# One third of a depthwise convolution moved from TensorE to ScalarE and GpSimd, in a kernel of dilated attention and binary convolution

## The chip, the cores and the metric

The kernel runs on one core of a Trainium2 chip, in float32 throughout except for the softmax weights, which are carried as three bfloat16 terms. The metric is the device time of one execution in microseconds (us), as the median of several runs. One execution was also taken by the hardware profiler; the profile that is shown below is of that execution. Engines are named as the profile names them: PE is TensorE's matmul, PEld its weight load, DVE is VectorE, ACT is ScalarE, POOL is GpSimd, SP is the engine whose queue issues nearly all transfers.

## The reference

The input x has the shape (16, 56, 56, 384): 16 images of 56 by 56 pixels with 384 channels. Two layers follow each other, each with a group norm ahead of it (32 groups of 12 channels, over all pixels of an image) and a residual sum behind it.

```python
# layer 0: dilated attention
x = x + attention(gn(x), w_qkv, w_proj, b_proj)
#   qkv = w_qkv applied per pixel; 3 groups of 128 channels with dilation 1, 2, 3;
#   4 heads of 32 channels per group; each pixel attends to its 9 dilated neighbours
# layer 1: depthwise 3x3 convolution with a binary kernel
x = x + conv(gn(x), w)
#   w_clip = clip(w, -1, 1);  k = w_clip + (sign(w_clip) - w_clip)
#   conv_general_dilated(x, k, padding='SAME', feature_group_count=384)
```

The change touches the second layer: every channel is convolved alone, with nine taps whose values are the signs of its weights.

## The kernel before, in words

**Tiling.** An image is cut into 7 slices of 8 rows (`PX` = 448 pixels); there are 112 slices in all. The channels lie on the partitions, as 3 groups of 128 (`NG`, index `g` or `j`). Three stages are run as a pipeline over slices, with scratch arrays in HBM between them. Stage A (`plan_a`) loads x, turns it by TensorE transposes, takes the sums for the first norm and writes `xd`. Stage B (`plan_b`) reads `xd` back, normalises it, computes k, v and q by matmuls of 128 x 448 (`pkv`, `pq`, line 337), multiplies q with three shifted views of k on DVE (`t`, L387), sums them over a head's channels on TensorE (`ps`, L371), takes the softmax, and then weighs v: for each of 27 pairs of group and tap a matmul spreads the weights over the partitions (`pb_a`, L443), DVE multiplies them with a shifted view of v (`w`, L446), and GpSimd adds the product to the group's sum (`y`, L453). The output projection (`po`, L467) and the residual follow, the sums for the second norm, and `x1d` is written. Stage C (`plan_c`) is the convolution.

**The convolution.** For each group j of 128 channels, `load` brings 4 sets of 32 channels into a tile `z` of 96 partitions. Each set lies there three times, shifted by one row (three transfers, L531). ScalarE normalises the four sets (L536). `convolve` then runs 12 matmuls for the group, three column shifts by four sets, with diagonal kernels `kdiag` of 96 x 32 as weights (L553). The profile counts each float32 matmul as two. The four sets of a shift go to different columns of the array, and the code keeps the twelve back to back. DVE adds the result to the slice of `x1d` that `load_x` brought (L560). `turn` transposes the sum back, ScalarE copies it out of PSUM (`osb`, L567), and a transfer writes it to the output.

**The order.** Pieces of the stages are entered in a table by a step and a rank (`at(when, order, piece)`), 9 steps to a slice; stage C of a slice runs 10 slices behind its stage B. The sorted table is only the order of priority. A scheduler places the instructions of each engine from it, by its own estimate of when they are ready, and the hardware then executes each engine's instructions in that order. DVE, ACT, POOL and the SP queue each wait at the head of their own line; so does PE for its matmuls.

**Buffers that the change and the prediction touch.** The pool `w_p` has 5 tiles: the DVE product five places later needs the tile that POOL's sum frees. `ps_bc` has 2 PSUM banks for `pb_a`. `ps_mt` has 4 banks, shared by most other matmul results. `z_p` has 3 tiles. Keys and values lie in `kv`, with `KV_SLOTS` = 3 slots by slice; besides its own 8 rows a slot has the halo rows above and below, copied by transfers between slots (L350, L351). `mr` holds mean and scale of a norm by channel, `mrz` the same in the layout of `z`.

Of the kernel before, what the change touches and what calls it, by code (L numbers as in the profile page):

```python
# [8 lines left out]
F32 = mybir.dt.float32  # L9
# [15 lines left out]
GN_CH = 12  # L25
GN_G = 32
NR = NG * HEADS * NTAP
KV_SLOTS = 3
TERMS = 3


# [1 line left out]
def dilated_attention_then_binary_conv(  # L33
# [24 lines left out]

    nc = tc.nc
    B, H, W, C = x.shape
    PX = ROWS * W
# [3 lines left out]
    SCALE = float(HD) ** -0.5  # L67
    DIL = (1, 2, 3)
    K3 = 3 * HD

    xf = x.rearrange("b h w c -> b (h w) c")
    of = out.rearrange("b h w c -> b (h w) c")
# [51 lines left out]

    spread = const.tile([NR, NTAP, P], BF16, name="spread")

    kdiag = const.tile([K3, 3, NG * NQ, HD], F32, name="kdiag")
    with tc.tile_pool(name="setup", bufs=1) as setup:
        wq_in = setup.tile([P, 9, C], F32, name="wq_in")
        nc.sync.dma_start(wq_in, w_qkv.rearrange("(t p) c -> p t c", p=P))  # L130
# [37 lines left out]
            )  # L168
        nc.vector.tensor_copy(spread, spread_f)


        kc = setup.tile([K3, 3, NG * NQ], F32, name="kc")
        nc.vector.tensor_scalar(kc, k_in, -1.0, 1.0, op0=ALU.max, op1=ALU.min)
        kp = setup.tile([K3, 3, NG * NQ], F32, name="kp")
        nc.vector.tensor_single_scalar(kp, kc, 0.0, op=ALU.is_gt)
        kn = setup.tile([K3, 3, NG * NQ], F32, name="kn")
        nc.vector.tensor_single_scalar(kn, kc, 0.0, op=ALU.is_lt)
        nc.vector.tensor_sub(kp, kp, kn)
        nc.vector.tensor_sub(kp, kp, kc)
        nc.vector.tensor_add(kp, kc, kp)  # L180
        eye3 = setup.tile([K3, HD], F32, name="eye3")
        nc.gpsimd.memset(eye3, 0.0)
        for ky in range(3):
# [4 lines left out]
        for kx in range(3):  # L188
            nc.vector.tensor_tensor(
                kdiag[:, kx],  # L190
                kp[:, kx].unsqueeze(2).to_broadcast([K3, NG * NQ, HD]),
                eye3.unsqueeze(1).to_broadcast([K3, NG * NQ, HD]),
                ALU.mult,
            )

# [8 lines left out]
    y_p = ctx.enter_context(tc.tile_pool(name="y_p", bufs=5))  # L204
    s_p = ctx.enter_context(tc.tile_pool(name="s_p", bufs=1))
    a_p = ctx.enter_context(tc.tile_pool(name="a_p", bufs=4))
    z_p = ctx.enter_context(tc.tile_pool(name="z_p", bufs=3))
    x1_p = ctx.enter_context(tc.tile_pool(name="x1_p", bufs=2))
    o_p = ctx.enter_context(tc.tile_pool(name="o_p", bufs=2))
    st_p = ctx.enter_context(tc.tile_pool(name="st_p", bufs=2))  # L210


    kv = []
    for g, d in enumerate(DIL):
        kv.append([])
        for s in range(KV_SLOTS):
            t = const.tile([P, 2, ROWS + 2 * d, W + 2 * d], F32, name=f"kv_{g}_{s}")
            nc.gpsimd.memset(t[:, :, :, 0:d], 0.0)
            nc.gpsimd.memset(t[:, :, :, W + d : W + 2 * d], 0.0)
            kv[g].append(t)  # L220

    def rows(ap):
        return ap.rearrange("p (r w) -> p r w", w=W)
# [97 lines left out]
    def plan_b(m, t0):  # L321

        b, c = divmod(m, NCH)
        slot, prev = m % KV_SLOTS, (m - 1) % KV_SLOTS
        had = {}

        def load_x():
# [12 lines left out]

        def k_or_v(g, which):

            d, cur, bef = DIL[g], kv[g][slot][:, which], kv[g][prev][:, which]
            pk = ps_mt.tile([P, 512], F32, tag="mt", name="pkv")
            project(pk, (1 + which) * C + g * P)
            nc.scalar.copy(cur[:, d : d + ROWS, d : d + W], rows(pk[:, :PX]))  # L346
            if c == 0:
                nc.gpsimd.memset(cur[:, 0:d, :], 0.0)
            else:
                nc.sync.dma_start(cur[:, 0:d, :], bef[:, ROWS : ROWS + d, :])  # L350
                nc.sync.dma_start(bef[:, ROWS + d : ROWS + 2 * d, :], cur[:, d : 2 * d, :])  # L351
            if c == NCH - 1:
                nc.gpsimd.memset(cur[:, ROWS + d : ROWS + 2 * d, :], 0.0)
# [24 lines left out]
        def score(i):  # L378

            g, ky = divmod(i, 3)  # L380
            d = DIL[g]
            qg = rows(had["q"][:, :PX])
            q3 = bass.AP(qg.tensor, qg.offset, [qg.ap[0], (0, 3), *qg.ap[1:]])
            kw = kv[g][slot][:, 0, ky * d : ky * d + ROWS, 0:W]
            k3 = bass.AP(kw.tensor, kw.offset, [kw.ap[0], (d, 3), *kw.ap[1:]])
            t = t_p.tile([P, 3, PX], F32, tag="t", name="t")
            nc.vector.tensor_tensor(t.rearrange("p k (r w) -> p k r w", w=W), q3, k3, ALU.mult)  # L387
            ready.extend((i * 3 + kx, t[:, kx, :]) for kx in range(3))
            if len(ready) >= NQ or i == 8:
                score_round()  # L390
# [47 lines left out]
        def weigh(p):  # L438

            g, o = divmod(p, NTAP)  # L440
            d, (ky, kx) = DIL[g], divmod(o, 3)
            pb = ps_bc.tile([P, 512], F32, tag="bc", name="pb_a")
            nc.tensor.matmul(pb[:, :PX], spread[:, o, :], had[f"a{g}"], start=True, stop=True)  # L443
            w = w_p.tile([P, PX], F32, tag="w", name="w")
            vw = kv[g][slot][:, 1, ky * d : ky * d + ROWS, kx * d : kx * d + W]
            nc.vector.tensor_tensor(rows(w), rows(pb[:, :PX]), vw, ALU.mult)  # L446
# [6 lines left out]
            nc.gpsimd.tensor_tensor(y, had["w0"] if o == 1 else y, w, ALU.add)  # L453
# [23 lines left out]
        def norm():  # L477
            mr = spread_stats(group_stats(stats1.pop(b)))

            mr1[b] = mrz = st_p.tile([K3, NG, NQ, 2], F32, tag="mrz", name="mrz")  # L480
            for ky in range(3):
                for q in range(NQ):
                    nc.sync.dma_start(mrz[ky * HD : (ky + 1) * HD, :, q, :], mr[q * HD : (q + 1) * HD, :, :])

        at(t0 - 18, LOADS, load_x)
        for j in range(NG):
# [20 lines left out]
    def plan_c(m, t0):  # L507
# [23 lines left out]
                nc.sync.dma_start(z[ky * HD : (ky + 1) * HD, :, lo:hi], by_set[:, :, q0 + lo : q0 + hi])  # L531

        def normalise(j):
            z = had[f"z{j}"]
            for q in range(NQ):
                nc.scalar.activation(  # L536
                    z[:, q], z[:, q], AF.Identity, bias=mr1[b][:, j, q, 0:1], scale=mr1[b][:, j, q, 1:2]
                )
            for edge in edges(j):
                nc.gpsimd.memset(edge, 0.0)  # L540

        def load_x():
            had["x1"] = x1 = x1_p.tile([P, NG, PX], F32, tag="x1", name="x1")
            nc.sync.dma_start(x1, chunk_of(x1d[b], c))

        def convolve(j):
            z = had.pop(f"z{j}")
# [67 lines left out]
```

## Time and profile before

| what | value |
|---|---|
| median of 3 runs | 6155.91 us (6143.2 to 6156.27) |
| the profiled execution, its own time | 6148.66 us |
| its span from the first to the last instruction | 6146.7 us |
| PE busy | 5892.8 us (96%), 30933 matmuls |
| DVE busy | 4420.6 us (72%) |
| POOL busy | 3364.3 us (55%) |
| ACT busy | 2270.5 us (37%) |
| mean granted TensorE clock | 0.961 |
| one slice, from 2000 to 4000 us (38 slices) | 52.6 us |

A busy share is an average over the whole span. A matmul's end is modelled in the trace, so the records of neighbouring matmuls overlap a little; what a group of them occupies is read from the distance between its start and the start of the next group. In a line of the list of groups, the part after the bar gives the total busy time and the mean duration of one instruction in ns, and the part after the second bar the idle time of the engine just before these instructions, with what ended it.

### The profile page before, as it was taken

How to read it: one execution, taken by the hardware profiler on the slowest of the kernel's cores; microseconds unless marked ns; L12 is line 12 of the kernel's file. 1: busy time of each engine (PE TensorE's matmuls, PEld its weight loads, DVE VectorE, ACT ScalarE, POOL GpSimd, SP SyncE). 2: the span in 40 equal slices, each digit the busy share in tenths (PEclk: the TensorE clock that was granted, in tenths of full speed). 3: DMA queues.
4: the chain of work that ended last, by engine and by line, in shares of the span. 5: the costliest groups of instructions: out<-in, count | busy, mean ns of one | idle time of the engine just before them, and what ended most of it. 6: DMA issues, size and time to landing. Idle time of an engine off the chain costs nothing. (4 is left out here: it accounts for less than half of the span.)

```text
span 6146.7 us, 90026 instructions
## 1 busy us (share of the span) xinstructions
PE 5892.8 (96%) x30933; PEld 2720.9 (44%) x30933; DVE 4420.6 (72%) x6431; ACT 2270.5 (37%) x4025; POOL 3364.3 (55%) x3375
## 2 busy tenths in 40 slices
PE   6989999999999999999999999999999999999986
PEld 3434444444444444444444444444444444444432
DVE  3767777777777777777777777777777777777760
ACT  2222333333333333334333333333334333333334
POOL 1656555555555555555555556555555555555650
PEclk7999999999999999999999999999999999999985
DMA  4323445554555455545554555555455554444445
GB/s 149 105 69 102 138 132 150 147 148 141 140 149 146 136 152 141 146 136 147 152 143 137 142 148 142 143 146 148 140 140 149 150 149 139 133 131 115 125 131 143
DMA packets 675072, 848.03 MB, mean 138 GB/s; under 512 B 179507, under 2 KB 674614, under 8 KB 674614
## 3 DMA queue, kind: packets, MB, share of 16 engines
q1 hardware_dynamic: 670608, 841.67, 48.8%
q8 instruction: 244, 4.00, 0.3%
q14 instruction: 214, 1.75, 0.1%
q10 hardware_dynamic: 4006, 0.61, 0.1%
HBM read 539.11 MB, written 231.21 MB: 125 GB/s over the span
## 5 line engine op out<-in xcount | busy, mean ns | idle before, releaser
L453 POOL TENSOR_TENSOR y<-y,w 128x448 f32<-128x448 f32 x2352 | 2675.0, 1137 | 1227.8 <-DVE w L446 1085.8
L446 DVE TENSOR_TENSOR w<-pb_a,kv 128x448 f32<-128x448 f32 x3024 | 1797.4, 616 | 479.0 <-PE pb_a L443 468.4
L337 PE MATMUL pkv<-xn,wqkvT 128*128 128x448 f32 x4032 | 1641.9, 542 | 0.0
L387 DVE TENSOR_TENSOR t<-pq,kv 128x1344 f32<-128x1344 f32 x1008 | 1545.9, 1547 | 86.6 <-PE pq L337 70.2
L337 PEld LDWEIGHTS pkv<-xn,wqkvT 128*128 128x128 f32 x4032 | 762.2, 190 | 622.7 <-issue 592.7
L536 ACT ACTIVATE z<-z,mrz 96x448 f32<-96x448 f32 x1344 | 939.2, 757 | 124.7 <-DMA z<-x1d 99.2
L553 PE MATMUL pc<-z,kdiag 96*32 96x440 f32 (+1 forms) x8064 | 924.3, 561 | 54.2 <-ACT z L536 32.0
L443 PE MATMUL pb_a<-aT,spread 108*128 108x448 bf16 x3024 | 929.5, 360 | 47.9 <-DVE w L446 38.5
L346 ACT COPY kv<-pkv 128x448 f32<-128x448 f32 x672 | 358.6, 534 | 1607.8 <-PE pkv L337 1607.4
L337 PE MATMUL pq<-xn,wqkvT 128*128 128x448 f32 x2016 | 904.5, 560 | 0.0
L467 PE MATMUL po<-y,wprojT 128*128 128x448 f32 x2016 | 828.6, 539 | 1.7 <-POOL y L453 1.7
L371 PE MATMUL ps<-t,sel 128*32 128x448 f32 x6048 | 781.1, 570 | 31.7 <-DVE var L255 15.9
L453 POOL TENSOR_TENSOR y<-w 128x448 f32<-128x448 f32 x336 | 382.9, 1139 | 724.6 <-DVE w L446 685.7
L560 DVE TENSOR_TENSOR x<-pc,x 128x448 f32<-128x448 f32 x336 | 209.8, 624 | 582.6 <-PE pc L553 581.9
L443 PEld LDWEIGHTS <-spread 108*128 108x128 bf16 x3024 | 238.0, 98 | 786.7 <-issue 730.1
L467 PEld LDWEIGHTS po<-y,wprojT 128*128 128x128 f32 x2016 | 382.1, 190 | 337.3 <-issue 305.8
L470 DVE SCALAR_TENSOR_TENSOR xr<-po,bias,xr 128x448 f32<-128x448 f32 x336 | 228.7, 681 | 407.5 <-PE po L467 401.8
L337 PEld LDWEIGHTS pq<-xn,wqkvT 128*128 128x128 f32 x2016 | 400.1, 200 | 260.8 <-issue 230.2
L553 PEld LDWEIGHTS pc<-z,kdiag 96*32 96x32 f32 x8064 | 265.7, 113 | 554.3 <-issue 463.3
L423 POOL TENSOR_TENSOR rest<-e,e 112x432 f32<-112x432 f32 x112 | 114.2, 1019 | 391.4 <-ACT e L422 375.1
L308 ACT COPY xa<-pt_x 128x448 f32<-128x448 f32 x336 | 179.0, 534 | 362.5 <-PE pt_x L304 355.0
L333 ACT ACTIVATE xn<-xn,mr 128x448 f32<-128x448 f32 x336 | 231.4, 751 | 202.8 <-DMA xn<-xd 145.9
(90 smaller groups left out, 3363.0 us busy)
## 6 DMA issues: line engine op xcount, KB each, us to landing
z<-x1d SPq DMA_DIRECT2D x912, 224.0 KB, 4.0
xin<-in_x_dram SPq DMA_DIRECT2D x112, 672.0 KB, 6.5
xd<-xa SPq DMA_DIRECT2D x336, 224.0 KB, 2.3
xn<-xd SPq DMA_DIRECT2D x112, 672.0 KB, 4.5
xr<-xd SPq DMA_DIRECT2D x112, 672.0 KB, 4.3
x1d<-xr SPq DMA_DIRECT2D x112, 672.0 KB, 3.1
x<-x1d SPq DMA_DIRECT2D x112, 672.0 KB, 5.0
out_dram<-osb SPq DMA_DIRECT2D x448, 168.0 KB, 2.3
```

What stands on the lines that cost most here:

```text
L333: nc.scalar.activation(xj, xj, AF.Identity, bias=mr0[b][:, j, 0:1], scale=mr0[b][:, j, 1:2])
L337: nc.tensor.matmul(dst[:, :PX], wqkvT[:, cc, o0 : o0 + P], had["xn"][:, cc, :], start=(cc == 0), stop=(cc == NG - 1))
L346: nc.scalar.copy(cur[:, d : d + ROWS, d : d + W], rows(pk[:, :PX]))
L371: return nc.tensor.matmul(had["ps"][32 * j : 32 * j + 32, :PX], sel[:, s0 : s0 + 32], tk, start=(i == 0), stop=(p + NQ >= NG * NTAP),)
L387: nc.vector.tensor_tensor(t.rearrange("p k (r w) -> p k r w", w=W), q3, k3, ALU.mult)
L443: nc.tensor.matmul(pb[:, :PX], spread[:, o, :], had[f"a{g}"], start=True, stop=True)
L446: nc.vector.tensor_tensor(rows(w), rows(pb[:, :PX]), vw, ALU.mult)
L453: nc.gpsimd.tensor_tensor(y, had["w0"] if o == 1 else y, w, ALU.add)
L467: nc.tensor.matmul(po[:, :PX], wprojT[:, g, j * P : (j + 1) * P], had[f"y{g}"], start=(g == 0), stop=(g == NG - 1))
L470: nc.vector.scalar_tensor_tensor(xr[:, j, :], po[:, :PX], bias[:, j : j + 1], xr[:, j, :], op0=ALU.add, op1=ALU.add)
L536: nc.scalar.activation(z[:, q], z[:, q], AF.Identity, bias=mr1[b][:, j, q, 0:1], scale=mr1[b][:, j, q, 1:2])
L553: return nc.tensor.matmul(pcr[q * HD : (q + 1) * HD, :, lo:hi], kdiag[:, kx, j * NQ + q, :], rows(z[:, q])[:, :, lo + kx - 1 : hi + kx - 1 ...
```

## The change

The convolution of the last 128 channels (j = 2) no longer uses `z`, `kdiag` and TensorE. Its slice is loaded once, 10 rows by 128 channels, into a tile `xg`. ScalarE normalises it into a padded tile `zg` and multiplies nine shifted views of it, each by the tap's sign of that channel (`taps_g`). GpSimd sums the nine products, in two additions of 1344 elements and two of 448, and adds the sum to the middle rows of `xg` in place (`sum_g`); `turn` reads them from there. The pieces have steps of their own in the table, from t0 - 4 to t0 + 8. The tile pool `m_p` for the products has two tiles of three products. The tile pool `z_p` goes from three tiles to two. Keys and values have separate tiles, with two slots for k and three for v. `mr1` keeps `mr` beside `mrz`.

```diff
-KV_SLOTS = 3
+K_SLOTS, V_SLOTS = 2, 3
...
+    JG = NG - 1
...
-    kdiag = const.tile([K3, 3, NG * NQ, HD], F32, name="kdiag")
+    ktap = const.tile([P, NTAP], F32, name="ktap")
+
+    kdiag = const.tile([K3, 3, JG * NQ, HD], F32, name="kdiag")
...
+        def binary(dst, k_raw):
...
+        binary(kp.rearrange("p k s -> p (k s)"), k_in.rearrange("p k s -> p (k s)"))
+        kg_in = setup.tile([P, NTAP], F32, name="kg_in")
+        nc.scalar.dma_start(kg_in, w_conv.rearrange("y x c m -> c (y x m)")[JG * P : (JG + 1) * P, :])
+        binary(ktap, kg_in)
...
-                kp[:, kx].unsqueeze(2).to_broadcast([K3, NG * NQ, HD]),
-                eye3.unsqueeze(1).to_broadcast([K3, NG * NQ, HD]),
+                kp[:, kx, : JG * NQ].unsqueeze(2).to_broadcast([K3, JG * NQ, HD]),
+                eye3.unsqueeze(1).to_broadcast([K3, JG * NQ, HD]),
...
-    z_p = ctx.enter_context(tc.tile_pool(name="z_p", bufs=3))
+    z_p = ctx.enter_context(tc.tile_pool(name="z_p", bufs=2))
     x1_p = ctx.enter_context(tc.tile_pool(name="x1_p", bufs=2))
+    xg_p = ctx.enter_context(tc.tile_pool(name="xg_p", bufs=2))
+    m_p = ctx.enter_context(tc.tile_pool(name="m_p", bufs=2))
     o_p = ctx.enter_context(tc.tile_pool(name="o_p", bufs=2))
...
     kv = []
-    for g, d in enumerate(DIL):
+    for which, slots in enumerate((K_SLOTS, V_SLOTS)):
         kv.append([])
-        for s in range(KV_SLOTS):
-            t = const.tile([P, 2, ROWS + 2 * d, W + 2 * d], F32, name=f"kv_{g}_{s}")
-            nc.gpsimd.memset(t[:, :, :, 0:d], 0.0)
-            nc.gpsimd.memset(t[:, :, :, W + d : W + 2 * d], 0.0)
-            kv[g].append(t)
+        for g, d in enumerate(DIL):
+            kv[which].append([])
+            for s in range(slots):
+                t = const.tile([P, ROWS + 2 * d, W + 2 * d], F32, name=f"{'kv'[which]}_{g}_{s}")
+                nc.gpsimd.memset(t[:, :, 0:d], 0.0)
+                nc.gpsimd.memset(t[:, :, W + d : W + 2 * d], 0.0)
+                kv[which][g].append(t)
+
+
+    zg = []
+    for s in range(2):
+        t = const.tile([P, ROWS + 2, W + 2], F32, name=f"zg_{s}")
+        nc.gpsimd.memset(t, 0.0)
+        zg.append(t)
...
         def k_or_v(g, which):
 
-            d, cur, bef = DIL[g], kv[g][slot][:, which], kv[g][prev][:, which]
+            d, slots = DIL[g], kv[which][g]
+            cur, bef = slots[m % len(slots)], slots[(m - 1) % len(slots)]
...
-            kw = kv[g][slot][:, 0, ky * d : ky * d + ROWS, 0:W]
+            kw = kv[0][g][m % K_SLOTS][:, ky * d : ky * d + ROWS, 0:W]
...
-            vw = kv[g][slot][:, 1, ky * d : ky * d + ROWS, kx * d : kx * d + W]
+            vw = kv[1][g][m % V_SLOTS][:, ky * d : ky * d + ROWS, kx * d : kx * d + W]
...
-            mr1[b] = mrz = st_p.tile([K3, NG, NQ, 2], F32, tag="mrz", name="mrz")
+            mrz = st_p.tile([K3, NG, NQ, 2], F32, tag="mrz", name="mrz")
             for ky in range(3):
                 for q in range(NQ):
                     nc.sync.dma_start(mrz[ky * HD : (ky + 1) * HD, :, q, :], mr[q * HD : (q + 1) * HD, :, :])
+            mr1[b] = mr, mrz
...
         def normalise(j):
-            z = had[f"z{j}"]
+            z, mrz = had[f"z{j}"], mr1[b][1]
             for q in range(NQ):
                 nc.scalar.activation(
-                    z[:, q], z[:, q], AF.Identity, bias=mr1[b][:, j, q, 0:1], scale=mr1[b][:, j, q, 1:2]
+                    z[:, q], z[:, q], AF.Identity, bias=mrz[:, j, q, 0:1], scale=mrz[:, j, q, 1:2]
...
         def load_x():
-            had["x1"] = x1 = x1_p.tile([P, NG, PX], F32, tag="x1", name="x1")
-            nc.sync.dma_start(x1, chunk_of(x1d[b], c))
+            had["x1"] = x1 = x1_p.tile([P, JG, PX], F32, tag="x1", name="x1")
+            nc.sync.dma_start(x1, chunk_of(x1d[b], c)[:, :JG])
...
+        lo, hi = (0 if c else 1), ROWS + (2 if c < NCH - 1 else 1)
+        zp = zg[m % 2]
+
+        def load_g():
+            had["xg"] = xg = xg_p.tile([P, ROWS + 2, W], F32, tag="xg", name="xg")
+            nc.sync.dma_start(
+                xg[:, lo:hi, :].rearrange("p r w -> p (r w)"),
+                x1d[b][JG * P : (JG + 1) * P, p0 + (lo - 1) * W : p0 + (hi - 1) * W],
+            )
+
+        def normalise_g():
+            if c == 0:
+                nc.gpsimd.memset(zp[:, 0], 0.0)
+            if c == NCH - 1:
+                nc.gpsimd.memset(zp[:, ROWS + 1], 0.0)
+            mr = mr1[b][0]
+            nc.scalar.activation(
+                zp[:, lo:hi, 1 : W + 1], had["xg"][:, lo:hi, :], AF.Identity,
+                bias=mr[:, JG, 0:1], scale=mr[:, JG, 1:2],
+            )
+
+        def taps_g(ky):
+            t = m_p.tile([P, 3, PX], F32, tag="m", name="m")
+            for kx in range(3):
+                o = 3 * ky + kx
+                nc.scalar.activation(
+                    rows(t[:, kx]), zp[:, ky : ky + ROWS, kx : kx + W], AF.Copy, scale=ktap[:, o : o + 1]
+                )
+            if ky == 0:
+                had["m"] = t
+            else:
+                nc.gpsimd.tensor_tensor(had["m"], had["m"], t, ALU.add)
+
+        def sum_g(kx):
+            t = had["m"]
+            if kx < 3:
+                nc.gpsimd.tensor_tensor(t[:, 0], t[:, 0], t[:, kx], ALU.add)
+            else:
+                mid = had["xg"][:, 1 : ROWS + 1, :].rearrange("p r w -> p (r w)")
+                nc.gpsimd.tensor_tensor(mid, t[:, 0], mid, ALU.add)
+
         def turn(s):
             pt = ps_mt.tile([P, 512], F32, tag="mt", name="pt_o")
+            mid = had["xg"][:, 1 : ROWS + 1, :].rearrange("p r w -> p (r w)")
             for j in range(NG):
-                nc.tensor.transpose(pt[:SUB, j * P : (j + 1) * P], had["x1"][:, j, s * SUB : (s + 1) * SUB], ident)
+                src = mid if j == JG else had["x1"][:, j]
+                nc.tensor.transpose(pt[:SUB, j * P : (j + 1) * P], src[:, s * SUB : (s + 1) * SUB], ident)
             osb = o_p.tile([SUB, C], F32, tag="osb", name="osb")
             nc.scalar.copy(osb, pt[:SUB, :C])
             nc.sync.dma_start(of[b, p0 + s * SUB : p0 + (s + 1) * SUB, :], osb)
 
+        at(t0 - 4, LOADS, load_g)
+        at(t0 - 1, NORM, normalise_g)
+        for ky in range(3):
+            at(t0 + 2 * ky, CONVOLVE, lambda ky=ky: taps_g(ky))
+        for kx in (1, 2, 3):
+            at(t0 + 5 + kx, CONVOLVE, lambda kx=kx: sum_g(kx))
         at(t0 - 1, LOADS, load_x)
-        for j in range(NG):
+        for j in range(JG):
             at(t0 - 4 + 3 * j, LOADS, lambda j=j: load(j))
             at(t0 - 1 + 3 * j, NORM, lambda j=j: normalise(j))
             at(t0 + 2 + 3 * j, CONVOLVE, lambda j=j: convolve(j))
```

More of the change, by code (lines that the diff above doesn't have):

```diff
@@ L169, in dilated_attention_then_binary_conv @@
         nc.vector.tensor_copy(spread, spread_f)
-        kc = setup.tile([K3, 3, NG * NQ], F32, name="kc")
-        nc.vector.tensor_scalar(kc, k_in, -1.0, 1.0, op0=ALU.max, op1=ALU.min)
-        kp = setup.tile([K3, 3, NG * NQ], F32, name="kp")
[L175 to L180, printed above, removed]
+        def binary(dst, k_raw):
+            kc = setup.tile(list(k_raw.shape), F32, tag="kc", name="kc")
+            nc.vector.tensor_scalar(kc, k_raw, -1.0, 1.0, op0=ALU.max, op1=ALU.min)
+            kn = setup.tile(list(k_raw.shape), F32, tag="kn", name="kn")
+            nc.vector.tensor_single_scalar(dst, kc, 0.0, op=ALU.is_gt)
+            nc.vector.tensor_single_scalar(kn, kc, 0.0, op=ALU.is_lt)
+            nc.vector.tensor_sub(dst, dst, kn)
+            nc.vector.tensor_sub(dst, dst, kc)
+            nc.vector.tensor_add(dst, kc, dst)
+        kp = setup.tile([K3, 3, NG * NQ], F32, name="kp")
+        binary(kp.rearrange("p k s -> p (k s)"), k_in.rearrange("p k s -> p (k s)"))
+        kg_in = setup.tile([P, NTAP], F32, name="kg_in")
+        nc.scalar.dma_start(kg_in, w_conv.rearrange("y x c m -> c (y x m)")[JG * P : (JG + 1) * P, :])
+        binary(ktap, kg_in)
         eye3 = setup.tile([K3, HD], F32, name="eye3")
@@ L323, in plan_b @@
         b, c = divmod(m, NCH)
-        slot, prev = m % KV_SLOTS, (m - 1) % KV_SLOTS
         had = {}
```

## The prediction, made before the changed kernel ran

> **What bounds the kernel now.** I read the list of busy time by engine first, then busy time by stretches, then the timeline of one slice, because a share over the whole span does not say which wait ends last.
>
> ```profile
> PE 5892.8 (96%) x30933; PEld 2720.9 (44%) x30933; DVE 4420.6 (72%) x6431; ACT 2270.5 (37%) x4025; POOL 3364.3 (55%) x3375
> ```
>
> The stretches show where PE is not full. Their columns are the stretch, its length, then busy us (and instructions) of PE, PEld, DVE, ACT and POOL, the granted clock, the DMA share and GB/s:
>
> ```profile
> 0.00:100.00 100.00, 39.87 (x184) 32.56 (x185) 25.69 (x54) 27.03 (x49) 16.76 (x88) 0.62 0.57 176
> 2000.00:3000.00 1000.00, 984.76 (x5254) 458.01 (x5255) 749.17 (x1088) 384.07 (x683) 566.49 (x560) 0.98 0.51 143
> 6000.00:6050.00 50.00, 34.90 (x198) 10.73 (x190) 4.37 (x7) 21.42 (x37) 0.00 (x0) 0.64 0.65 161
> ```
>
> In the middle, PE is idle 1.5% of the time, and a slice takes 52.6 us (2736 convolution matmuls from 2000 to 4000 us, 72 to a slice, are 38 slices). By these shares a slice holds 39.4 us of DVE, 20.2 of ACT, 29.8 of POOL. So PE sets the pace there. At the end only stage C is left and no engine is full. Since PE is in order and full, what a convolution costs is the distance from its start to the next start on PE:
>
> ```profile
> 2999.73 2.44 PE L553 MATMUL pc<-z,kdiag 96*32 96x448 f32 x24
> 3002.10 0.36 PE L443 MATMUL pb_a<-aT,spread 108*128 108x448 bf16 x1
> ...
> 3042.70 2.42 PE L337 MATMUL pkv<-xn,wqkvT 128*128 128x448 f32 x6
> 3044.96 0.35 PE L443 MATMUL pb_a<-aT,spread 108*128 108x448 bf16 x1
> ...
> 3054.97 0.35 PE L443 MATMUL pb_a<-aT,spread 108*128 108x448 bf16 x1 [0.19 <-DVE w L446]
> ```
>
> The 24 matmuls of one group occupy 2.37 us (2.35 and 2.36 at 3015.89 and 3049.92), though the list of groups gives 561 ns for each: four run side by side. The last row is the weak place: PE waits for DVE at `pb_a`, and DVE can wait for POOL through the five `w` tiles. POOL already comes in bursts, seven additions in 8.46 us, or 1.21 each:
>
> ```profile
> 3002.26 1.03 POOL L423 TENSOR_TENSOR rest<-e,e 112x432 f32<-112x432 f32 x1 [4.39 <-ACT e L422]
> 3005.30 8.46 POOL L453 TENSOR_TENSOR y<-y,w 128x448 f32<-128x448 f32 x7
> ```
>
> [...] the 0.19 us at `pb_a` pass with other PE work behind it, so a late `w` stops everything on PE. [...] DVE's large operations here (L387, L446) [...] do not disturb POOL: its addition lasts 1122 to 1157 ns in 2000 us, so I let neither slow the other.
>
> **The change, part by part.** The sum is made against the profiled execution's own 6148.7 us (span 6146.7 and 2 us around it). The median of the runs, 6155.9, is 0.12% above it; I leave the sum as it is. A difference under 0.2% (12 us) is no difference that a measurement of this kernel could tell.
>
> *PE.* One of three convolutions goes, 24 matmuls and 2.36 us per slice. The profile's last 217 us hold 652 convolution matmuls, 9 slices; the other 103 slices run with PE full, so 103 x 2.36 = 243 us is the most to gain there. Transposes are as many as before.
>
> *ACT.* Four L536 go (2.72 us in a row on the timeline). Added are one normalise of 560 elements and nine products of 448. [...] Nine and one make 6.0 us, 3.2 more per slice, to 23.4 of 51. This is hidden where PE is full, except for its latency (below).
>
> *POOL.* Added are two additions of 1344 elements and three of 448 (1.21 each, 3.6). [...] at most 3 x 1137 = 3.4. Sum 9.7 us per slice: 39.5 of 51, 77%. It has the time, but not always when it is wanted.
>
> *Costed at nothing.* DVE loses 0.62 us (L560). SP loses three z issues of 0.42 us and gains one for `xg`; that one stands behind `osb` and `xa` stores, whose wait for ACT is counted below. Transfers shrink. k's second slot: a k tile is planned 4 steps, 23 us, after the last read of the slice two before. `z_p` with two tiles for two groups keeps one tile per group as before. Setup adds a transfer, six short DVE operations and memsets inside the first 100 us, where POOL is 83% and PE 60% idle; 0 to 10 us, taken as 0.
>
> *Where the pieces land.* The steps in the table are only priorities. In the order of the changed kernel's instructions the nine products stand together on ACT, right behind the normalise, and POOL's five sums stand among only three `y` additions. They are not spread. Since `m_p` has two tiles, the third three products need the tile that the first large addition frees: ACT waits for POOL, then POOL for ACT, with `y` additions queued behind on POOL and copies out of PSUM behind on ACT. I count from the last transpose of a `turn` (3013.6). The store of `xa` that `xg`'s load follows was issued 2.2 us later; so its issue is at 2.6, and it lands 4.2 later (the median of the transfers of `xr`) at 6.8. Normalise and six products take 4.3, the large addition 3.05, three products 1.8, the second addition 3.05, then y, sum, y, sum, sum, y: 6 x 1.21 = 7.3, and four hand-overs of 0.08 (POOL started 0.08 after ACT's cast at 3002.26): 26.6. This last `y` frees the tile for the DVE product five places on. PE reaches that product's `pb_a` after 20 pairs of large matmuls (0.753 each, from the row at 3042.70), 15 pairs of `ps` (0.22), one convolution, 15 `pb_a` (0.19) and 1.0 of transposes: 24.6; DVE could start it at 25.3. It starts at 26.6, ends at 27.2, and frees the bank that PE wants at 26.6. **PE stalls 0.6 us.** Bounds: with a landing of 3.1 us nothing is left; with 6.7 (the extremes of `xr`) and 3.4 us additions it is 3.8. I take 0.9 per slice, as lateness counts in full and earliness only to zero. POOL then recovers at 51/27 = 1.9 us per `pb_a` against 1.21 before the softmax.
>
> *The end.* There a slice takes 217 / 9 = 24 us, bound by load, normalise and convolution in turn at a lower clock. Afterwards one `z` tile goes round once a slice: load 4.0, issue 0.4, normalise 2.7, convolution 4.65 (at 6059.41), and ACT's 6.0 for the third group and about 1 for `osb` between: 19 us. Gain 5 x 9 = 45; from 0 (no overlap) to 70 (ACT alone, 16 us).
>
> Sum: 103 x (2.36 - 0.9) = 150, and 45: **5954 us**, rounded to 5955.
>
> **The rivals.**
> *All hidden:* `xg` lands early, no stall. 243 + 45 gives 5861. For it: POOL's average of 77%, and a worked stall that is small. Against it: in-order queues with no slack left. Chance 0.22.
> *Forecast:* stall below 1.8 us, 5955. Chance 0.45.
> *Most of it given back:* a stall of 1.8 to 2.8 us, 6046 to 6149. Chance 0.19, of which 0.07 within 0.2%.
> *Slower:* ACT and POOL wait for each other over the two `m` tiles, and each microsecond of that goes through `w` to PE. It decides from 2.36 + 45/103 = 2.8 us per slice. At the bound of 3.8, 103 x 1.44 = 148 us are lost and 45 gained at the end: 6252. For it: every link is in the order of instructions, and the landing times reach far enough. Against it: it needs nearly the worst of each. Chance 0.14.
> That the work isn't spread as the words say is part of all four.
>
> **How the numbers follow.** Faster 0.22 + 0.45 + 0.12 = 0.79, same 0.07, slower 0.14. The range goes from 5850, a little below the case without stall for a better end, up to 6130, where some 0.17 is left above. The cases of a gain alone would span 5850 to 6046.
>
> **What would show it.** Convolution matmuls should fall to 5376 and PE's busy time by a third of 924, to about 5585 us. Products should last some 650 ns, large additions 3.0 to 3.4 us. PE's waits for DVE's `w`, and DVE's for POOL's `y`, should appear at the sums, about 90 us in all, and the last nine slices should be shorter. If PE's idle share in the middle stays at 1.5%, the first rival is right. If it rises above 6%, the last one is.

## The result: slower by 0.4%, and the profile after

| | kernel before | changed kernel |
|---|---|---|
| median of the runs, us | 6149.56 (4 runs) | 6170.45 (4 runs) |
| ratio, 95% interval | | 1.0036 [1.0016, 1.0056] |
| profiled execution, us | 6148.66 | 6178.98 |
| its span, us | 6146.7 | 6177.3 |

The interval leaves out 1, so the change costs 21 us by the medians. Small as it is, every run of the changed kernel (6164.8 us at least) was longer than every run of the kernel before beside it (6156.3 at most). The work itself moved as the diff says. The list of busy time by engine of the changed kernel:

```profile
PE 5714.0 (93%) x28245; PEld 2662.7 (43%) x28245; DVE 4379.2 (71%) x6325; ACT 2644.9 (43%) x4697; POOL 4388.1 (71%) x3917
```

PE lost 2688 matmuls and 179 us of busy time, and the span grew all the same: PE was idle 254 us before and 463 us after. The same stretches as before (length, busy us and instructions of PE, PEld, DVE, ACT and POOL, granted clock, DMA share, GB/s):

```profile
2000.00:3000.00 1000.00, 951.50 (x4776) 446.80 (x4774) 739.52 (x1070) 447.87 (x797) 737.98 (x648) 0.97 0.47 131
6000.00:6050.00 50.00, 22.51 (x128) 7.21 (x120) 2.50 (x4) 23.87 (x41) 19.76 (x15) 0.60 0.44 118
```

In the middle PE is now idle 4.85% of the time instead of 1.5%, on a kernel in which nothing else was full. The groups of the changed kernel say what it waits for (count, busy us and mean ns of one, then the idle time ahead of the group and what ended it):

```profile
L467 DVE TENSOR_TENSOR w<-pb_a,v 128x448 f32<-128x448 f32 x3024 | 1796.0, 616 | 692.8 <-PE pb_a L464 420.3 <-POOL y L474 261.6 <-PE pt_s L421 2.2
...
L464 PE MATMUL pb_a<-aT,spread 108*128 108x448 bf16 x3024 | 949.0, 362 | 152.2 <-DVE w L467 143.1 <-DVE dev L269 0.8 <-DVE var L276 0.6
...
L615 POOL TENSOR_TENSOR m<-m 128x1344 f32<-128x1344 f32 x224 | 680.5, 3038 | 356.1 <-ACT m L609 333.1 <-DVE w L467 9.6 <-DVE var L276 7.0
...
L609 ACT ACTIVATE m<-zg,ktap 128x448 f32<-128x448 f32 x1008 | 592.2, 658 | 383.9 <-POOL m L615 377.7 <-POOL xg L623 2.5
```

Read from the bottom up, this is a chain. ACT's products wait 378 us for POOL, POOL's large additions wait 333 us for ACT, DVE waits 262 us for a `w` tile that POOL's `y` has not read yet (3.0 us before), and PE waits 143 us for DVE (38.5 before). How it happens stands in the timeline of POOL and ACT in one ordinary slice (start, duration, engine, line; `x` is the number in a row; the bracket is the idle time before it and its releaser):

```profile
3038.13 3.47 ACT L609 ACTIVATE m<-zg,ktap 128x448 f32<-128x448 f32 x6
3044.75 1.79 ACT L609 ACTIVATE m<-zg,ktap 128x448 f32<-128x448 f32 x3 [3.15 <-POOL m L615]
```

```profile
3041.68 3.03 POOL L615 TENSOR_TENSOR m<-m 128x1344 f32<-128x1344 f32 x1 [1.55 <-ACT m L609]
3044.67 1.14 POOL L474 TENSOR_TENSOR y<-y,w 128x448 f32<-128x448 f32 x1
3046.68 3.05 POOL L615 TENSOR_TENSOR m<-m 128x1344 f32<-128x1344 f32 x1 [0.87 <-ACT m L609]
3049.67 1.15 POOL L474 TENSOR_TENSOR y<-y,w 128x448 f32<-128x448 f32 x1
3050.77 1.14 POOL L620 TENSOR_TENSOR m<-m 128x448 f32<-128x448 f32 x1
3051.86 1.15 POOL L474 TENSOR_TENSOR y<-y,w 128x448 f32<-128x448 f32 x1
3052.95 1.15 POOL L620 TENSOR_TENSOR m<-m 128x448 f32<-128x448 f32 x1
3054.18 1.14 POOL L623 TENSOR_TENSOR xg<-m,xg 128x448 f32<-128x448 f32 x1
3055.27 1.13 POOL L474 TENSOR_TENSOR y<-w 128x448 f32<-128x448 f32 x1
```

From 3041.68 to 3055.27, 13.6 us, POOL gives the five sums 9.5 us of work and gets three `y` done. POOL finds ACT not ready at both large additions, ACT finds POOL not ready for its third three products. POOL took nothing ahead of the waiting addition: the `w` that DVE had ended at 3043.02 lay ready in the 0.87 us before the second one, and its `y` came behind it, at 3049.67.

**Where the time went by stretch.** A slice is measured from the start of one `rest` (POOL L444) to the next; an image has seven slices. Two of the seven are long, about 59 us: the statistics of the normalisation are worked out in them, a chain through DVE, PE and ACT. The table is the mean of 13 images, from slice 14 to 105, and the stretches around it, in us:

| kernel | five ordinary slices | two long slices | an image | last `rest` to last `po` | last `po` to the end |
|---|---|---|---|---|---|
| before | 248.7 | 118.4 | 367.1 | 46.6 | 191.7 |
| changed | 242.1 | 124.7 | 366.8 | 61.1 | 191.5 |

The ordinary slices gained 6.6 us per image. The long ones lost 6.3, and nothing was left. Over the 13 images that is a gain of 3.5 us. The span still grew by 30.6 us, because the rest lost: 7.2 us up to the first `rest`, 4.9 in the first 14 slices, 7.8 in the last six, 14.5 from there to the last `po`; after it 0.2 were gained.

One such loss in a long slice, in the timeline of the changed kernel:

```profile
2797.98 0.36 PE L464 MATMUL pb_a<-aT,spread 108*128 108x448 bf16 x1
2798.40 1.13 POOL L623 TENSOR_TENSOR xg<-m,xg 128x448 f32<-128x448 f32 x1
2799.49 1.13 POOL L474 TENSOR_TENSOR y<-w 128x448 f32<-128x448 f32 x1
...
2800.65 0.62 DVE L467 TENSOR_TENSOR w<-pb_a,v 128x448 f32<-128x448 f32 x1 [4.66 <-POOL y L474]
...
2801.32 0.35 PE L464 MATMUL pb_a<-aT,spread 108*128 108x448 bf16 x1 [2.99 <-DVE w L467]
```

POOL ran the last sums ahead of a `y` whose `w` had been ready since 2795.98; DVE stood 4.66 us and PE 2.99 us behind it. The statistics stand behind such waits on DVE too: PE's `pp` (L292), which needs DVE's `pair`, waited 42.4 us in all, 8.5 before:

```profile
PE pp L292 <- DVE pair L284: 42.4, 16, 3.5
```

### The profile page after: what moved, and what is told of

Same layout as the page of the kernel before. It is cut to its first block, busy times and chain, and to the rows that moved or that the text cites. A ratio compares the mean times of both kernels' runs of the same rounds, so it can differ in the third digit from the quotient of the medians.

```text
span 6177.3 us, 85206 instructions
## 1 busy us (share of the span) xinstructions
PE 5714.0 (93%) x28245; PEld 2662.7 (43%) x28245; DVE 4379.2 (71%) x6325; ACT 2644.9 (43%) x4697; POOL 4388.1 (71%) x3917
## 5 line engine op out<-in xcount | busy, mean ns | idle before, releaser
L467 DVE TENSOR_TENSOR w<-pb_a,v 128x448 f32<-128x448 f32 x3024 | 1796.0, 616 | 692.8 <-PE pb_a L464 420.3
L357 PE MATMUL pkv<-xn,wqkvT 128*128 128x448 f32 x4032 | 1684.0, 554 | 0.0
L408 DVE TENSOR_TENSOR t<-pq,k 128x1344 f32<-128x1344 f32 x1008 | 1545.8, 1547 | 99.5 <-PE pq L357 87.5
L464 PE MATMUL pb_a<-aT,spread 108*128 108x448 bf16 x3024 | 949.0, 362 | 152.2 <-DVE w L467 143.1
L615 POOL TENSOR_TENSOR m<-m 128x1344 f32<-128x1344 f32 x224 | 680.5, 3038 | 356.1 <-ACT m L609 333.1
L609 ACT ACTIVATE m<-zg,ktap 128x448 f32<-128x448 f32 x1008 | 592.2, 658 | 383.9 <-POOL m L615 377.7
L575 PE MATMUL pc<-z,kdiag 96*32 96x440 f32 (+1 forms) x5376 | 578.8, 566 | 81.9 <-ACT z L558 46.3
L558 ACT ACTIVATE z<-z,mrz 96x448 f32<-96x448 f32 x896 | 626.1, 759 | 31.0 <-DMA z<-x1d 31.0
L582 DVE TENSOR_TENSOR x<-pc,x 128x448 f32<-128x448 f32 x224 | 139.7, 624 | 395.1 <-PE pc L575 395.1
L367 ACT COPY v<-pkv 128x448 f32<-128x448 f32 x336 | 176.6, 526 | 555.0 <-PE pkv L357 555.0
L353 ACT ACTIVATE xn<-xn,mr 128x448 f32<-128x448 f32 x336 | 233.1, 754 | 289.4 <-DMA xn<-xd 181.0
```

Source lines behind the costliest of these rows:

```text
L353: nc.scalar.activation(xj, xj, AF.Identity, bias=mr0[b][:, j, 0:1], scale=mr0[b][:, j, 1:2])
L357: nc.tensor.matmul(dst[:, :PX], wqkvT[:, cc, o0 : o0 + P], had["xn"][:, cc, :], start=(cc == 0), stop=(cc == NG - 1))
L558: nc.scalar.activation(z[:, q], z[:, q], AF.Identity, bias=mrz[:, j, q, 0:1], scale=mrz[:, j, q, 1:2])
L575: return nc.tensor.matmul(pcr[q * HD : (q + 1) * HD, :, lo:hi], kdiag[:, kx, j * NQ + q, :], rows(z[:, q])[:, :, lo + kx - 1 : hi + kx - 1 ...
L609: nc.scalar.activation(rows(t[:, kx]), zp[:, ky : ky + ROWS, kx : kx + W], AF.Copy, scale=ktap[:, o : o + 1])
L615: nc.gpsimd.tensor_tensor(had["m"], had["m"], t, ALU.add)
```

## The experiments

Three theories were set against each other. **A:** POOL's sums come in a row ahead of `y` additions, and the wait passes through the five `w` tiles to DVE and PE; part of it is the mutual wait of ACT and POOL over the two `m` tiles. **B:** ACT's added work, or its waiting for POOL, delays its copies out of PSUM and the normalise of `z`, and PE waits for ACT. **C:** something else in the change (k in two slots, the load, setup) costs what PE saved. In all ratios below the kernel before ran beside the kernel tried; its medians in the five sessions of this document lay between 6148.1 and 6153.3 us, so a difference under some 5 us between kernels of two sessions tells nothing.

### The third group left out

The normalise, the products and the sums of the third group are left out, so its convolution is missing from the output; `xg`'s load, the `turn` and k's two slots stay.

```
-        at(t0 - 1, NORM, normalise_g)
-        for ky in range(3):
-            at(t0 + 2 * ky, CONVOLVE, lambda ky=ky: taps_g(ky))
-        for kx in (1, 2, 3):
-            at(t0 + 5 + kx, CONVOLVE, lambda kx=kx: sum_g(kx))
```

> Leaves out of the changed kernel the normalise, the nine products and all five sums of the third group; its slice is still loaded and turned. It is the bound of what taking the matmuls away can bring. Theory A (GpSimd's sums hold back y, and through w PE): all 2.36 us of each slice are gained, the two long slices of an image (59 us before, 62 after) come down to about 57, total near 5900 us. Theory B (ScalarE's chain of load, normalise and products is what holds PE) gives the same here. Theory C (two slots for k make the long slices longer): the long slices stay near 62 us less 2.4, total near 5980.

Measured: 5904.0 us, 0.9603 [0.9584, 0.9623]. The 244 us against the kernel before are what PE can save; C falls, since k's slots and the load are in it. The changed kernel gives back 266 us. The traces show where PE lost them: in all, PE waited for DVE 112.6 us here and 256.8 in the changed kernel, for ACT 30.1 and 56.6, for POOL 54.6 and 78.2.

### ACT alone, and POOL alone

*Products without sums:* ACT makes all nine products, POOL adds none of them, and the sum is missing from the output.

```
-            if ky == 0:
-                had["m"] = t
-            else:
-                nc.gpsimd.tensor_tensor(had["m"], had["m"], t, ALU.add)
...
-        for kx in (1, 2, 3):
-            at(t0 + 5 + kx, CONVOLVE, lambda kx=kx: sum_g(kx))
```

> Leaves out GpSimd's five sums per slice; ScalarE still normalises and forms the nine products, which nobody reads. Theory A: as without the third group, near 5900 us, GpSimd busy near 3370 us. Theory B (ScalarE's late copies and its 6 us at a stretch delay PE): near 6170 us.

Measured: 5910.6 us, 0.9614 [0.9595, 0.9633]. ACT's 6 us per slice cost 6.6 us in the whole kernel, so B falls as far as it is ACT's work. ACT waits for nobody here, so its waiting for POOL is not tested by this run; that part of B is bounded by PE's waits for ACT, which grew by 26.5 us in the changed kernel, and by the run with ten `w` tiles below.

*Sums without products:* POOL makes the five additions on two constant tiles of zeros; normalise and products are left out, and the third group's convolution is missing from the output.

```
-            t = m_p.tile([P, 3, PX], F32, tag="m", name="m")
...
+                had["m"] = mz[0]
             else:
-                nc.gpsimd.tensor_tensor(had["m"], had["m"], t, ALU.add)
+                nc.gpsimd.tensor_tensor(had["m"], had["m"], mz[1], ALU.add)
```

> Leaves out ScalarE's normalise and products; GpSimd does the same five sums, on two tiles that are set to zero once, at about the same places among its y additions, and never waits for ScalarE. Theory A in its plain form (the 9.7 us of work are too much where they stand): most of the loss stays, 6100 to 6170 us. Theory A in the form of my prediction (the mutual wait of ScalarE and GpSimd over the two m tiles lets the burst start late and stretches it): most of the loss goes, 5900 to 5960 us. Theory B: near 5900 us.

Measured: 6035.9 us, 0.9819 [0.9805, 0.9834], between the ranges expected. POOL's additions, which stand in a row here too but have nothing to wait for from ACT, cost 132 us over the kernel without the third group, half of the loss. This is not a clean part of the loss, though: POOL's order is another one, and its last addition, ahead of the others in it, waits for the load of `xg` (244 us in all, 79 times), which in the changed kernel is ACT's wait. The other 135 us of the changed kernel come with ACT's part in the same tiles.

### A third `m` tile

```
-    m_p = ctx.enter_context(tc.tile_pool(name="m_p", bufs=2))
+    m_p = ctx.enter_context(tc.tile_pool(name="m_p", bufs=3))
```

> The changed kernel with a third buffer for the products, nothing else: ScalarE may write the next row of taps while GpSimd still adds the last two, which should take most of the 378 us in which ScalarE waited for an m buffer. Theory A (half of the loss is the mutual wait of ScalarE and GpSimd): about 6040 us, between 6035 (the kernel with sums alone) and 6100. Theory B (what costs is the place and the amount of GpSimd's sums, ahead of the y additions that TensorE waits for through w): within 20 us of the changed kernel, 6150 to 6190. In A the two long slices of an image fall from 124.7 us to about 119; in B they stay.

Measured: 6054.6 us, 0.9843 [0.9828, 0.9857], as A has it. ACT's wait for POOL's large additions is gone from the list of waits, and POOL's for ACT fell from 333 to 219 us (total us, times, longest):

```profile
POOL m L615 <- ACT m L609: 219.0, 85, 8.8
...
DVE w L467 <- POOL y L474: 153.7, 116, 6.5
...
PE pb_a L464 <- DVE w L467: 98.0, 134, 4.9
```

This one edit is worth 116 us and turns the change from 0.4% slower to 1.6% faster. The long slices fell to 119.5 us per image. But the edit is not the buffer alone: with three tiles the scheduler also placed POOL's instructions differently (565 of 3917 places, the two large additions next to each other in most slices; PE and DVE keep their order). How the 116 us divide between the third tile and the new order is not shown.

### Ten `w` tiles, in both kernels

```
-    w_p = ctx.enter_context(tc.tile_pool(name="w_p", bufs=5))
+    w_p = ctx.enter_context(tc.tile_pool(name="w_p", bufs=10))
```

In the changed kernel:

> The changed kernel with 10 tiles of w in place of 5, nothing else. Theory A: GpSimd may fall ten products behind before DVE and PE notice; the stalls at pb_a in the ordinary slices go and most of those in the long slices, 5920 to 6000 us. Theory B or C: no change, near 6170 us.

Measured: 5996.2 us, 0.9755 [0.9739, 0.9771], as A has it. In the traces the instructions of PE, DVE, ACT and POOL stand in the same order in both kernels, so only the number of tiles differs. ACT and POOL still wait for each other as before, and PE's wait for `w` fell from 143 to 61 us (total us, times, longest):

```profile
ACT m L609 <- POOL m L615: 377.4, 112, 16.2
...
POOL m L615 <- ACT m L609: 338.1, 182, 9.8
...
PE pb_a L464 <- DVE w L467: 61.0, 103, 2.1
...
DVE w L467 <- POOL y L474: 22.6, 24, 9.2
```

This shows the path most directly: with the same waits of ACT for POOL, 378 and 377 us, five `w` tiles cost 174 us that ten don't. PE's waits for ACT are still there (56.6 us with five tiles, 55.0 with ten), so what B can be worth is not in these 174 us. The control is the kernel before with ten:

> The kernel before with ten w buffers and no other edit: the control for ten buffers in the changed kernel. In the kernel before TensorE waited for DVE at pb_a for 47.9 us in all. Theory A (the buffers are worth something because the new sums delay y): at most 40 us here, 6110 to 6150, so that the change is worth 110 us or more once w is deep. Theory B (deep w is worth as much without the change): about 6000, and then the change itself still brings nothing.

Measured: 6153.4 us, 1.0003 [0.9994, 1.0011], no gain, where A allowed 40 us at most and B had about 6000. Without the sums a deeper `w` is worth nothing.

*Seven `w` and three `m`* in the changed kernel, in the same memory as ten `w`:

> The changed kernel with seven w and three m buffers, its own turns: the two buffers in the same memory as ten w. Theory A (the middle needs w deep enough for 9.7 us of sums, the end needs the third m): the middle as with ten w, the end as with three m, 5970 to 5990. Theory B (seven w are too few for five sums in a row): 6010 to 6040, between the third m alone (6055) and ten w (5996).

Measured: 6000.7 us, 0.9756 [0.9742, 0.9771], between the two ranges expected: an image takes 355.5 us (354.1 with ten `w`), the end 173.3 (190.8).

### The pieces in program order

The steps at which the change puts its pieces are priorities, and the order of the instructions does not keep them: in it the nine products stand in a row. Here each product and each sum is kept in program order on its engine, and nothing else in the code is changed:

```
-                nc.scalar.activation(
+                tc.keep_in_program_order(nc.scalar.activation(
...
-                nc.gpsimd.tensor_tensor(had["m"], had["m"], t, ALU.add)
+                tc.keep_in_program_order(nc.gpsimd.tensor_tensor(had["m"], had["m"], t, ALU.add))
...                                          (likewise both additions in sum_g)
```

> The changed kernel with products and sums held in program order on their engines, at the turns where the change puts them (nothing moved, five w and two m buffers): it separates the fixed order from the spreading. Theory A (it is the spreading that recovered the middle): within 40 us of the changed kernel, 6130 to 6210. Theory B (the fixed order alone recovers it, the turns chosen matter little): about 6000.

Measured: 5972.7 us, 0.9708 [0.9692, 0.9724], the fastest of all kernels with the full computation: 178 us below the kernel before and 198 below the changed one. Theory A as it was put there, that the turns themselves must be moved, falls. The fixed order is enough, and in it the pieces are at last spread. (The scheduler also shifted some of the other instructions, 325 of 28245 places on PE and 180 of 6325 on DVE; what that is worth was not tested apart.) POOL in one slice of this kernel:

```profile
3044.22 3.04 POOL L615 TENSOR_TENSOR m<-m 128x1344 f32<-128x1344 f32 x1
3047.34 1.14 POOL L620 TENSOR_TENSOR m<-m 128x448 f32<-128x448 f32 x1
3048.41 0.27 POOL L548 MEMSET z<- 32x224 f32 x1
3048.65 7.20 POOL L474 TENSOR_TENSOR y<-y,w 128x448 f32<-128x448 f32 x6
3055.81 1.14 POOL L620 TENSOR_TENSOR m<-m 128x448 f32<-128x448 f32 x1
...
3060.91 1.13 POOL L474 TENSOR_TENSOR y<-w 128x448 f32<-128x448 f32 x1 [3.77 <-DVE w L467]
```

The first large addition of this slice ran at 3022.58, more than 20 us earlier, and no sum here waits for ACT. After the sums POOL is early again: it waits for DVE. ACT's wait for the load of `xg` also fell, from 264 to 93 us. The four waits of the chain (total us, times, longest):

```profile
POOL m L615 <- ACT m L609: 87.0, 39, 10.5
...
PE pb_a L464 <- DVE w L467: 68.1, 111, 1.9
...
DVE w L467 <- POOL y L474: 20.2, 30, 4.9
...
ACT m L609 <- POOL m L615: 17.5, 4, 6.1
```

*The order kept and the turns moved* (load at `t0 - 1`, normalise at `t0 + 2`, rows of taps at `t0 + 3`, `+ 5` and `+ 7`, sums at `t0 + 8` to `+ 10`, `turn` two later), and the same with ten `w` or three `m`:

> The changed kernel with the products and sums held in program order on their engines, and the pieces moved so that each addition of 3.0 us stands between other y additions of its slice instead of all five standing together: the load one turn before the slice, the normalise at turn 2, the rows of taps at 3, 5, 7, the sums at 8, 9, 10, TensorE's own turn two turns later. Theory A (five sums in a row, 9.7 us, hold back three y additions until w runs out): spread, each holds back one y by 3 us, which five w buffers cover; the middle falls to about 355 us per image and the time to 5950 to 6030. Theory B (GpSimd has too little room in the two long slices wherever the sums stand): 6120 to 6200. Theory C (a fixed order makes GpSimd wait on ScalarE's late products with y additions queued behind): over 6200.

> As the spread order, with ten w buffers instead of five: the two remedies together. If both act on the same wait (DVE for a w buffer, and TensorE behind DVE), about the time of ten buffers alone, 5980 to 6000; if the spread order takes a different part, the end among it, 5930 to 5970. Over 6050 if the fixed order brings a wait of its own that no buffer covers.

> The spread order with a third m buffer, five w buffers. In the spread order ScalarE waited only 22 us for an m buffer in all, so in the middle the third buffer is worth nothing; in the last stage, where the pieces of one slice have no y additions between them, the stretch from the last po to the end is 195 us there and 174 with three m buffers in the changed order. Theory A (the last stage is bound by ScalarE and GpSimd alternating on two m buffers): 5970 to 5985. Theory B (in the spread order the later turn sets the last stage): no difference, 5990 to 6000.

Measured: 5998.1 us, 0.9754 [0.9739, 0.9768], as A has it; with ten `w` 5993.6, 0.9746 [0.9730, 0.9762]; with three `m` 5986.4, 0.9732 [0.9717, 0.9746]. Ten `w` saved 4 us in a spread order and 174 in the order of the change: spreading and deep `w` act on the same wait. The third `m` tile gained 12 us, all of it after the last `po` (195.1 to 183.3); the 5986.4 lie a little above the 5970 to 5985 that A had.

*The order kept, seven `w` and three `m`:*

> The fixed order at the turns of the change, with seven w and three m buffers besides: what is left after the order. Left over the kernel without the third group (5904 us) are some 69 us: 2.6 us in each of 14 images, 27 us after the last po, 12 us ahead of it. Theory A (the rest is still the rows of sums against w and m buffers): the middle at 352 to 353 us per image and the end at about 172, 5935 to 5955. Theory B (the fixed order already took what the buffers can give in the middle; what is left there is GpSimd's own work in front of y in the long slices): the middle stays at 354 to 355 and only the end gains, 5960 to 5970.

Measured: 5976.8 us, 0.9711 [0.9695, 0.9727], no different from the order alone, the end included (181.0 and 181.2). The middle is as B has it; that the end would gain was wrong in both theories.

**Side by side**, from the same stretches as the first table, in us:

| kernel | ordinary | long | an image | last `rest` to `po` | `po` to end | median |
|---|---|---|---|---|---|---|
| third group left out | 238.0 | 113.9 | 351.9 | 46.5 | 154.2 | 5904.0 |
| products without sums | 237.9 | 113.7 | 351.6 | 46.5 | 163.7 | 5910.6 |
| sums without products | 238.8 | 119.2 | 358.0 | 65.0 | 162.7 | 6035.9 |
| three `m` | 239.6 | 119.5 | 359.1 | 65.1 | 173.5 | 6054.6 |
| ten `w` | 238.3 | 115.8 | 354.1 | 60.8 | 190.8 | 5996.2 |
| program order | 237.4 | 117.1 | 354.5 | 58.6 | 181.2 | 5972.7 |
| changed kernel | 242.1 | 124.7 | 366.8 | 61.1 | 191.5 | 6170.5 |

What remains between the program order and the kernel without the third group, 69 us, lies in the long slices (3.2 per image), after the last `po` (27.0) and ahead of it (12.1). What sets those was not settled; that the third `m` tile shortens the end with the turns moved and not with the order alone is open too.

## Why the prediction was wrong

It forecast 5955 us and faster; 6170 lies above its range, on the side to which it gave 0.14.

**Right: the prices.** A product lasts 658 ns (some 650 in the prediction), a large addition 3.04 us (3.05), and the five sums take 9.5 us (9.7). The nine products and the normalise keep ACT busy for 6.1 us per slice (6.0), 0.84 of them the normalise. Nothing in the kernel before shows these prices; the prediction's were the author's estimates, and the runs bear them out. That neither DVE nor POOL slows the other held too: with POOL busy 71% of the span instead of 55%, a `w` on DVE still lasts 616 ns and a `y` on POOL 1137. "Costed at nothing" held for k's second slot, DVE and ACT's time.

**A little too high: what PE can save.** With nothing lost the prediction had 243 + 45, or 5861 us. The kernel without the third group's work on any engine takes 5904. An ordinary slice got 2.14 us shorter in it (10.7 / 5), not 2.36, and the stretch after the last `po` 37.5, not 45. That 103 x 2.36 = 243 comes so close to the 244 us of the whole kernel is chance. Why 2.36 became 2.14 is open.

**Right: the path.** "Where the pieces land" named it link by link: not spread, the third products waiting for POOL, POOL for ACT, `y` behind, then `w`, DVE and `pb_a`. In the slice shown above the last transpose of the `turn` ended at 3030.14. From there the normalise of `xg` began at 7.1 us (6.8 in the prediction), and the `y` behind the last sum was done at 26.3 (26.6):

```profile
3029.87 0.27 PE L630 MATMUL pt_o<-ident,xg 128*112 128x128 f32 x1
...
3037.23 0.86 ACT L600 ACTIVATE zg<-xg,mr 128x560 f32<-128x560 f32 x1 [2.58 <-DMA xg<-x1d]
```

That the forecast meets this one slice so closely has some luck in it: loads of `xg` kept ACT waiting for up to 6.8 us.

**Wrong: "I take 0.9 per slice", for all 103.** For ordinary slices it is close. Leaving the third group out gains 10.7 us on five of them, the change 6.6, so each loses 0.8. But two slices in seven lose far more: 124.7 against 113.9, 5.4 each. The prediction's one alignment was read from an ordinary slice. In a long one DVE also carries the statistics behind its wait for `w`, and PE waits for those as well. The traces divide the 5.4 us: against the kernel without the third group PE is idle 3.2 us longer in a long slice, 1.4 of them ahead of `pb_a` and 1.8 at the matmuls of the statistics (`pp` above all), and it is busy 2.2 us longer with the same matmuls, at a mean granted clock of 0.91 instead of 0.95. The prediction had no term for waits at the statistics or for slower matmuls. Over the 13 images counted the stall is 26 x 4.5 = 117 us above the forecast, half of the miss. It is above even the upper bound of 3.8.

**Wrong: "The end: gain 45".** After the last `po` it was 0.2. The forecast let ACT's six microseconds lie one after the other with nothing between. The timeline of the last stage shows what came between:

```profile
6123.22 3.02 POOL L615 TENSOR_TENSOR m<-m 128x1344 f32<-128x1344 f32 x1 [9.67 <-ACT m L609]
...
6126.27 1.78 ACT L609 ACTIVATE m<-zg,ktap 128x448 f32<-128x448 f32 x3 [2.40 <-POOL m L615]
...
6127.96 3.36 ACT L558 ACTIVATE z<-z,mrz 96x448 f32<-96x448 f32 x5
...
6130.71 1.72 PE L575 MATMUL pc<-z,kdiag 96*32 96x448 f32 x8 [7.55 <-ACT z L558]
```

ACT waits 2.40 us for POOL at the third products, and the next `z` normalise, for which PE waits 7.55 us, stands behind them, at 6127.96. It is the mutual wait again, at a place where no `w` stands between. Against the kernel before (191.7 us) this stretch gained 37.5 us without the third group's work, 28.0 with the products alone, 18.2 with everything and three `m` tiles, and 0.2 with two.

**Not counted: the stretch ahead of it, the start and setup.** From the last `rest` to the last `po` 14.5 us were lost, in the six slices before 7.8, and in the first 14 slices 4.9, where the prediction's sum had gains of 1.46 per slice. The kernel with sums alone loses the first as well (65.0 us), and the one with products alone does not (46.5), so it is POOL's work. Setup was taken at 0 out of 0 to 10: the first `rest` came at 155.6 us instead of 148.4, but at 152.2 in the kernel before with ten `w` tiles too, so up to half of the 7.2 is not the change's.

**The rivals and the signs.** The last rival had the mechanism, the mutual wait that goes through `w` to PE. Its size was wrong the other way: it decided from 2.8 us in every slice, while the mean over ordinary and long slices is (5 x 0.8 + 2 x 5.4) / 7 = 2.1. That the kernel came out slower is due to the stretches before and after the 13 images, where the 45 us were not gained and 34 were lost. PE's idle share in the middle, 4.85%, fell between the two marks set (1.5% and 6%), so this sign decided nothing. PE's wait for `w` at `pb_a` rose by 105 us, near the 90 forecast. PE's busy time fell by 179 us, not by 308: the convolution matmuls themselves are down by 345 (924.3 to 578.8), but some of that was overlapped, and the other matmuls took longer (last section).

## What to carry to other kernels

Work that is moved to an engine with room to spare is hidden only if each piece stands where that engine's other results are not yet wanted, and that is read from the order of its instructions, not from the steps one wrote: here the order alone turned 0.4% slower into 2.9% faster. Where two in-order engines pass tiles to each other, try one tile more than they hold at a time (the third `m`, with the order that came with it, was worth 116 us here, and nothing on top of the program order with seven `w`), and look at how many tiles lie between them and the engine that sets the pace (ten `w` instead of five were worth 174). A stall worked out in one slice holds for slices of its kind only; find the slices that carry other work, and work it out there too.

## What the runs showed of the hardware that was not expected

Some waits of PE cost more than their own length here: the matmuls after them were slower. At the end of the image loop, in the timeline of PE of the changed kernel:

```profile
5956.24 0.53 PE L464 MATMUL pb_a<-aT,spread 108*128 108x448 bf16 x1 [3.67 <-DVE w L467]
5961.31 1.06 PE L464 MATMUL pb_a<-aT,spread 108*128 108x448 bf16 x2 [4.53 <-DVE w L467]
...
5964.18 4.66 PE L575 MATMUL pc<-z,kdiag 96*32 96x448 f32 x24
...
5981.90 4.85 PE L488 MATMUL po<-y,wprojT 128*128 128x448 f32 x6 [5.99 <-POOL y L474]
```

After waits of 3.67 and 4.53 us close together, 24 matmuls of `pc` took 4.66 us instead of 2.44, and after 5.99 us six `po` took 4.85, while six large matmuls took 2.42 in the stretch around 3042 us of the kernel before. The granted clock was 1.00 from 5945 to 5954 us and 0.50 from 5957 to 5969. After the single wait of 2.99 us at 2801.32 six `pkv` took 2.42, at a granted clock of 1.00. In the kernel before, 24 `pc` were as slow with no wait of such a length ahead of them:

```profile
5939.46 0.35 PE L443 MATMUL pb_a<-aT,spread 108*128 108x448 bf16 x1 [0.68 <-DVE w L446]
5940.67 0.53 PE L443 MATMUL pb_a<-aT,spread 108*128 108x448 bf16 x1 [0.86 <-DVE w L446]
5941.13 4.66 PE L553 MATMUL pc<-z,kdiag 96*32 96x448 f32 x24
```

From 5930 to here no wait of PE was longer than 0.86 us, but PE was busy only 2.10 of the 4 us from 5936 to 5940, and from 5940 to 5946 the granted clock was 0.50. So here the clock fell behind several short waits close together; what decides when it falls was not measured.

Between 1000 and 5000 us, of some 5485 large matmuls, 196 lasted over 0.6 us in the changed kernel and 118 before, and their excess over 0.55 us was 68 and 31 us. Over the whole span the same 28245 matmuls kept PE busy for 5714.0 us in the changed kernel and for 5634.8 without the third group: of the 277 us between the spans of these two, 198 are idle time of PE and 79 slower matmuls.
